# Key product by seven half products, with the activations held by halves of the tokens

## The chip, the cores and the metric

The kernel runs on one core of a Trainium2 chip. The metric is the device time of one execution in microseconds. It is taken without the profiler. Everything is computed in 32-bit floats; on TensorE one such matmul shows in the trace as two MATMUL records and two weight loads.

## The reference, cut to what matters

Four sequences (B = 4) of T = 512 tokens with H = 512 channels pass through an adaptive layer norm, an RWKV block (time mixing, then channel mixing), a second adaptive layer norm and a mixture of experts. The change lies in the channel mixing:

```python
h = _layer_norm(x, ln2_g, ln2_b)
hh = _time_shift(h)
kk = (h * cm_mk + hh * (1 - cm_mk)) @ Wkey.T        # 512 -> FF = 2048
kv = jax.nn.silu(kk) @ Wval.T                       # 2048 -> 512
sr = jax.nn.sigmoid((h * cm_mr + hh * (1 - cm_mr)) @ Wcr.T)
x = x + sr * kv
```

The key product is `kk`, the value product is `kv`.

## The kernel before, in words

**Order.** Each engine runs its instructions strictly in the order in which the Python source issues them. `weave(main, back)` sets that order: each time the main generator yields, one step of the back generator is put in. Around the change the main generator is `channel_mix(b)`, for b = 0 to 3, and the back generator is `channel_front(b + 1)` (norm, turn and mixes for the next sequence, 11 steps) followed by `channel_back(b - 1)` (second norm, router and slot tables of the previous sequence, 17 steps). At b = 0 there is only the front, at b = 3 only the back. Of the back's steps two are long on VectorE: step 13 picks the experts, and step 15 builds `at_slot` and `at_row`, which the matmuls of step 16 (`ps_rows`) read.

**Stages of channel_mix(b).** First come four gate products `ps_cr` with `wcr`; at b = 0 the four output products `o_steps(3)` of time mixing stand among them, and they begin with `flush()`, which issues the last division (`L364`, `L365`) on VectorE and, behind it, the last multiplication `av` (`L366`) on GpSimd. Then 16 chunks of 128 rows of f follow. `project` (`L323`) multiplies a chunk of `wkey` by the four tiles `xk` of 128 channels by 512 tokens: four matmuls of 512 columns into a bank `ps_kk`. ScalarE takes the sigmoid (`L541`), VectorE multiplies (`L542`) into the tile `s` of 512 tokens, and from chunk 8 on adds half of it to an earlier tile (`L546`). The banks of tag "ps" are four, so that a chunk may wait for three others before TensorE needs its bank again.

**The value product** is already made of seven products of halves, in `product` (`L562`), with three banks X, Y and Z, 32 MATMUL records of 256 columns each. The sums of the quarters of `wval` that it needs are made once, at b = 0, by `sum_step` (`L500`), one step in each chunk, and stored to `sums_d` (`L504`) for the later sequences. `minus` (`L576`) makes the differences of activations while the products run.

**Loads.** All DMAs except the gathers are issued by SyncE, in order, and an issue that has to wait holds up the ones behind it. Weights live in a pool of 8 tiles of 1 MB (`wpool`). `load_key` (`L94`) fetches 1 MB of `wkey` for four chunks, one group ahead; `get(0)`, called at f = 13, fetches the first quarter of `wval` for the value product.

Of the kernel before, what the change touches and what calls it, by code (L numbers as in the profile page):

```python
# [8 lines left out]
F32 = mybir.dt.float32  # L9
I32 = mybir.dt.int32  # L10
AF = mybir.ActivationFunctionType
# [3 lines left out]
P = 128  # L15
B, T, H = 4, 512, 512
NT = T // P
NK = H // P
FF = 4 * H
NF = FF // P  # L20
NG = FF // H
# [23 lines left out]
def adaln_block(  # L45
# [22 lines left out]
    nc = tc.nc  # L68
# [3 lines left out]
    wpool = ctx.enter_context(tc.tile_pool(name="w", bufs=8))  # L72
# [5 lines left out]
    def bank(name, tag="ps"):  # L78
        return psum.tile([P, 512], F32, tag=tag, name=name)

    def row_tile(name, shape=(P, H)):

        return tpool.tile(list(shape), F32, tag="t", name=name)
# [4 lines left out]
    def load_w(src, name, parts=1):  # L88

        w = w_tile(name)  # L90
        n = NK // parts
        rows = src.rearrange("(k p) o -> p k o", p=P)
        for i in range(parts):
            nc.sync.dma_start(w[:, i * n : (i + 1) * n, :], rows[:, i * n : (i + 1) * n, :])  # L94
        return w
# [224 lines left out]
    def project(w, acts, m, ps):  # L320

        for k in range(NK):
            nc.tensor.matmul(ps, w[:, k, m * P : (m + 1) * P], acts[k], start=(k == 0), stop=(k == NK - 1))  # L323
# [143 lines left out]

    h3_d = dram.tile([N, H], F32, tag="h3_d", name="h3_d")
    h3s = [None] * B
    wkey = {}  # L470


    HT, NF2 = T // 2, NF // 2
    (B11, B12, B21, B22, T1, T2, T3, T4) = range(8)
    sums_d = dram.tile([4, P, NF2 * HT], F32, tag="sums_d", name="sums_d")
    quarters, wsum = {}, {}

    def load_key(b, g):
        wkey[b, g] = load_w(wkey_t[:, g * H : (g + 1) * H], f"wkey_{b}_{g}")

    def load_quarter(b, q):
        w = wpool.tile([P, NF2, HT], F32, tag="w", name=f"wval_{b}_{q}")
# [7 lines left out]

    def sum_step(n):


        q, part = divmod(n, 4)
        if n == 0:
            for i in (B12, B11, B22, B21):
                wsum[i] = load_quarter(0, i)
        dst, one, other = ((B11, B12, B11), (B12, B22, B12), (B22, B22, B11), (B21, B21, B22))[q]
        at = slice(part * NF2 // 4, (part + 1) * NF2 // 4)
        nc.vector.tensor_sub(wsum[dst][:, at, :], wsum[one][:, at, :], wsum[other][:, at, :])  # L500
        if part == 3:
            i = (T1, T3, T2, T4)[q]
            quarters[0, i] = wsum[dst]
            nc.sync.dma_start(sums_d[i - T1].rearrange("p (k o) -> p k o", k=NF2), wsum[dst])  # L504

    def channel_mix(b):

        xk, xr = channel_mixes[b][CK], channel_mixes[b][CR]
        x1, ga = x1s[b], spread(GA, b)
        srs, xres = [], []  # L510
        for t in range(NT):
            ps = bank(f"ps_cr_{b}_{t}")
            project_tokens(wcr, xr, t, ps)
            yield
            sr = row_tile(f"sr_{b}_{t}")
            nc.scalar.activation(sr, ps, AF.Sigmoid)
            nc.gpsimd.tensor_mul(sr, sr, ga)
            srs.append(sr)
            if b == 0 and t == 1:
                yield from o_steps(B - 1)  # L520
            if t == 0:
                xres = [load_x(b, i, f"xr_{b}_{i}") for i in range(NT)]
            else:
                nc.gpsimd.tensor_mul(x1[t - 1], x1[t - 1], ga)
                nc.gpsimd.tensor_add(x1[t - 1], x1[t - 1], xres[t - 1])
        nc.gpsimd.tensor_mul(x1[NT - 1], x1[NT - 1], ga)
        nc.gpsimd.tensor_add(x1[NT - 1], x1[NT - 1], xres[NT - 1])

        ss = []
        order_of = (B11, T2, T1, B21, T3, B22, T4)  # L530

        def get(n):
            if n < len(order_of) and (b, order_of[n]) not in quarters:
                quarters[b, order_of[n]] = load_quarter(b, order_of[n])

        for f in range(NF):
            ps = bank(f"ps_kk_{b}_{f}")
            project(wkey[b, f // NK], xk, f % NK, ps)
            yield
            s = row_tile(f"s_{b}_{f}", (P, T))  # L540
            nc.scalar.activation(s, ps, AF.Sigmoid)  # L541
            nc.vector.tensor_mul(s, s, ps)  # L542
            ss.append(s)
            if f >= NF2:

                nc.vector.tensor_add(ss[f - NF2][:, HT:], ss[f - NF2][:, HT:], s[:, HT:])  # L546
            if b == 0:
                sum_step(f)
            if f % NK == 1 and f // NK + 1 < NG:
                load_key(b, f // NK + 1)  # L550
            if f >= NF - 4 and f % 2:
                get((f - NF + 3) // 2)

        def product(q, rows, col, ps, fresh, done=None):


            w = quarters.pop((b, q))
            for half in range(2):
                chunks = range(half * NF2 // 2, (half + 1) * NF2 // 2)
                for i in chunks:  # L560
                    for j in range(2):
                        nc.tensor.matmul(  # L562
                            ps[:, j * HT : (j + 1) * HT],
                            ss[rows + i][:, col + j * P : col + (j + 1) * P],
                            w[:, i, :],
                            start=(fresh and i == 0 and j == 0),
                            stop=(i == NF2 - 1 and j == 1),
                            skip_group_check=True,
                        )
                yield  # L570
                if done is not None:
                    for i in chunks:
                        done(i)

        def minus(dst, one, other):
            nc.vector.tensor_sub(dst, one, other)  # L576

        def result(t0, col, part):

            at = slice(col, col + HT)  # L580
            for j in range(2):
                t = t0 + j
                nc.vector.tensor_mul(srs[t][:, at], srs[t][:, at], part[:, j * HT : (j + 1) * HT])
                nc.vector.tensor_add(x1[t][:, at], x1[t][:, at], srs[t][:, at])


        X = bank(f"ps_x_{b}", "acc")
        get(2)
        yield from product(B11, 0, 0, X, True, lambda i: minus(ss[i][:, :HT], ss[i][:, HT:], ss[i][:, :HT]))
        c1 = row_tile(f"c1_{b}")  # L590
        nc.scalar.activation(c1, X, AF.Copy)

        Y = bank(f"ps_y_{b}", "acc")
        get(3)
        yield from product(T2, 0, 0, Y, True)
        u2 = row_tile(f"u2_{b}")
        nc.vector.tensor_add(u2, c1, Y)

        Z = bank(f"ps_z_{b}", "acc")
        get(4)  # L600
        yield from product(T1, 0, HT, Z, True, lambda i: minus(ss[i][:, HT:], ss[NF2 + i][:, HT:], ss[i][:, :HT]))
        c5 = row_tile(f"c5_{b}")
        nc.scalar.activation(c5, Z, AF.Copy)  # L603
        nc.gpsimd.tensor_add(c5, c5, c1)  # L604

        get(5)
        yield from product(
            B21, NF2, 0, X, False, lambda i: minus(ss[NF2 + i][:, :HT], ss[NF2 + i][:, :HT], ss[i][:, :HT])
        )
        result(0, 0, X)  # L610

        get(6)
        yield from product(T3, 0, HT, Y, False)
        nc.vector.tensor_add(c5, c5, Y)
        result(2, HT, c5)

        if b + 1 < B:
            load_key(b + 1, 0)
        yield from product(B22, NF2, 0, Z, False)
        nc.vector.tensor_add(u2, u2, Z)  # L620
        result(0, HT, u2)

        yield from product(T4, NF2, HT, Y, False)
        nc.vector.tensor_add(c1, c1, Y)
        result(2, 0, c1)
        channel_mixes[b] = None
# [444 lines left out]
    def weave(main, back, plan=()):  # L1071

        plan = iter(plan)
        for _ in main:
            for _ in range(next(plan, 1)):
                next(back, None)
# [5 lines left out]
    def chained(*parts):  # L1082
        for p in parts:
            yield from p()
# [42 lines left out]
    for b in range(1, B):  # L1127
        if b + 1 < B:
            back = chained(lambda: time_front(b + 1))
        else:  # L1130
            wcr = load_w(wcr_t, "wcr")
            load_key(0, 0)
            back = channel_front(0, "acc")
        weave(time_mix(b), back)
        drain(back)
    nc.sync.dma_start(router[:, :, :E_RT], w_router.rearrange("(k p) e -> p k e", p=P))
    for b in range(B):
        parts = []
        if b + 1 < B:
            parts.append(lambda: channel_front(b + 1, "ps"))  # L1140
        if b >= 1:
            parts.append(lambda: channel_back(b - 1))
        back = chained(*parts)
        weave(channel_mix(b), back)
        drain(back)
        if b == 0:
            clear_rest()
# [36 lines left out]
    for b in (B - 2, B - 1):  # L1184
        for t in range(NT):
            ps = down_bank(b, t)
# [51 lines left out]
```

## Time and profile before

| what | value |
| --- | --- |
| median of 3 runs | 1068.97 us (1068.79 to 1070.17) |
| the profiled execution, time | 1077.15 us |
| its span, first to last instruction | 1075.4 us |
| granted TensorE clock, mean | 0.988 |
| TensorE busy | 1043.0 us, 97% of the span |
| VectorE busy | 602.2 us, 56% |
| ScalarE busy | 284.0 us, 26% |
| GpSimd busy | 276.0 us, 26% |
| key products `ps_kk`, all four sequences | 225.4 us of TensorE |
| value products, ps_x + ps_y + ps_z | 57.3 + 84.8 + 57.0 us of TensorE |

The profiled execution is longer than the median by 8.2 us, so a sum made in the trace is compared with 1077.15 us, and only the difference is carried over to the median. In the rows of the trace "[1.19 <-DVE at_row L830]" says that the engine stood idle for 1.19 us before that row and that VectorE's instruction of line 830 ended the wait. "128x256 f32 x32" are 32 records of that shape. Line numbers of the profile are those of the kernel before.

In the trace the four key stages lie at 295 to 351, 413 to 473, 538 to 598 and 664 to 728 us from the start of the span, and each value stage follows its key stage.

### The profile page before, as it was taken

To read this page: it belongs to the slowest core of one execution; us is meant where nothing else is said; L and a number is where in the kernel's file an instruction comes from. 1 tells how busy PE (TensorE), PEld (TensorE's weight loads), DVE (VectorE), ACT (ScalarE), POOL (GpSimd) and SP (SyncE) were. 2 spreads that over 40 slices of the span, in tenths; PEclk is the share of its full clock that TensorE was granted. 3 is DMA by queue.
4 is the path that set the end of the run, shared out by engine and by line. 5 is a ranking of instruction groups with operands and counts; after the bars stand their busy time and mean duration, and the time that the engine had idled before them with its cause. 6 is when DMAs were issued, how large, how long until landed. Compare 5 with 4: busy or idle time off the path is not lost. (4 is left out here: it accounts for less than half of the span.)

```text
span 1075.4 us, 10261 instructions
## 1 busy us (share of the span) xinstructions
PE 1043.0 (97%) x3440; PEld 597.2 (56%) x3440; DVE 602.2 (56%) x1158; ACT 284.0 (26%) x459; POOL 276.0 (26%) x274
## 2 busy tenths in 40 slices
PE   7998989999999999999999999999999999999997
PEld 2443434444444884468644785448845666656643
DVE  5886998867464444747446576274456222224327
ACT  1744453534231004320152101311030222113210
POOL 2453463523430006100231006100013222141250
PEclk9998999999999999999999999999999999999999
DMA  8700130024024560084204611915242899899853
GB/s 313 236 1 2 39 99 0 1 84 135 27 78 157 171 230 1 29 316 134 59 1 150 232 40 41 347 43 190 65 156 84 283 381 382 302 320 311 290 181 109
DMA packets 93607, 161.77 MB, mean 150 GB/s; under 512 B 6552, under 2 KB 44952, under 8 KB 91504
## 3 DMA queue, kind: packets, MB, share of 16 engines
q1 hardware_dynamic: 87712, 141.95, 38.4%
q0 software_dynamic: 5840, 19.14, 5.6%
q8 instruction: 28, 0.46, 0.2%
q14 instruction: 27, 0.22, 0.1%
HBM read 136.11 MB, written 24.95 MB: 150 GB/s over the span
## 5 line engine op out<-in xcount | busy, mean ns | idle before, releaser
L323 PE MATMUL ps_kk<-mix_ln,wkey 128*128 128x512 f32 x512 | 225.4, 596 | 0.0
L323 PEld LDWEIGHTS ps_kk<-mix_ln,wkey 128*128 128x128 f32 x512 | 96.3, 191 | 114.1 <-issue 112.2
L202 POOL TENSOR_TENSOR rstd_ln<-rstd_ln,minus_half 128x1 f32<-128x1 f32 x64 | 40.0, 625 | 232.9 <-DVE rstd_ln L201 220.4
L542 DVE TENSOR_TENSOR s<-s,ps_kk 128x512 f32<-128x512 f32 x64 | 44.0, 687 | 99.4 <-ACT s L541 99.3
L562 PE MATMUL ps_y<-wval,s 128*128 128x256 f32 x384 | 84.8, 379 | 0.0
L541 ACT ACTIVATE s<-ps_kk 128x512 f32<-128x512 f32 x64 | 38.2, 597 | 158.8 <-PE ps_kk L323 153.1
L1009 PE MATMUL ps_down<-wrt,at 128*128 128x512 f32 x164 | 78.9, 604 | 1.0 <-issue 1.0
L993 PE MATMUL ps_up<-wrt,xt 128*128 128x256 f32 x328 | 77.9, 380 | 1.3 <-DVE xt L987 1.3
L562 PEld LDWEIGHTS ps_y<-wval,s 128*128 128x128 f32 x384 | 72.8, 190 | 9.8
L246 DVE SCALAR_TENSOR_TENSOR mix_ln<-hT_ln,inv,mix_ln 128x511 f32<-128x511 f32 x64 | 61.7, 1006 | 24.2 <-ACT mix_ln L240 24.2
L970 POOL DMA_INDIRECT xg<-h_d,token x41 | 39.3, 959 | 126.4 <-PE ps_down L1009 42.6
L328 PE MATMUL ps_o<-wo,av 128*128 128x512 f32 x128 | 59.5, 619 | 4.7 <-POOL av L366 4.1
L993 PEld LDWEIGHTS ps_up<-wrt,xt 128*128 128x128 f32 x328 | 59.1, 190 | 8.8 <-DVE xt L987 2.4
L604 POOL TENSOR_TENSOR c<-c,c 128x512 f32<-128x512 f32 x4 | 5.1, 1286 | 226.2 <-ACT c L603 184.4
L323 PE MATMUL ps_r<-mix_ln,wr 128*128 128x512 f32 x128 | 59.3, 607 | 0.1
L987 DVE COPY xt<-ps_xt 128x512 f32<-128x512 f32 x41 | 28.3, 689 | 55.0 <-PE ps_xt L985 43.1
L323 PE MATMUL ps_v<-mix_ln,wv 128*128 128x512 f32 x128 | 58.1, 597 | 0.0
L562 PE MATMUL ps_x<-wval,s 128*128 128x256 f32 x256 | 57.3, 380 | 0.0
L915 PE MATMUL ps_up_sh<-h,wsh 128*128 128x512 f32 x128 | 57.2, 593 | 0.0
L562 PE MATMUL ps_z<-wval,s 128*128 128x256 f32 x256 | 57.0, 379 | 0.0
L929 PE MATMUL ps_down_sh<-wsh,mid 128*128 128x512 f32 x128 | 56.3, 594 | 0.4 <-PEq L1180 0.4
L328 PE MATMUL ps_cr<-wcr,mix_ln 128*128 128x512 f32 x128 | 55.9, 592 | 0.0
(195 smaller groups left out, 1487.3 us busy)
## 6 DMA issues: line engine op xcount, KB each, us to landing
wrt<-in_rt_up_dram SPq DMA_DIRECT2D x41, 512.0 KB
wrt<-in_rt_down_dram SPq DMA_DIRECT2D x41, 512.0 KB
wkey<-in_wkey_t_dram SPq DMA_DIRECT2D x16, 1024.0 KB
wval<-in_wval_t_dram SPq DMA_DIRECT2D x16, 1024.0 KB
wval<-sums_d SPq DMA_DIRECT2D x12, 1024.0 KB
y_d<-y SPq DMA_DIRECT2D x41, 256.0 KB
mod<-mod_d SPq DMA_DIRECT2D x22, 256.0 KB
x<-in_x_dram SPq DMA_DIRECT2D x16, 256.0 KB
```

The costliest lines, as they stand in the source:

```text
L202: nc.gpsimd.tensor_tensor(rstd, rstd, minus_half, ALU.pow)
L246: nc.vector.scalar_tensor_tensor(t[:, 1:], hT[:, : T - 1], inv[:, m - MK, k : k + 1], t[:, 1:], ALU.mult, ALU.add)
L323: nc.tensor.matmul(ps, w[:, k, m * P : (m + 1) * P], acts[k], start=(k == 0), stop=(k == NK - 1))
L328: nc.tensor.matmul(ps, acts[k][:, t * P : (t + 1) * P], w[:, k, :], start=(k == 0), stop=(k == NK - 1))
L541: nc.scalar.activation(s, ps, AF.Sigmoid)
L542: nc.vector.tensor_mul(s, s, ps)
L562: nc.tensor.matmul(ps[:, j * HT : (j + 1) * HT], ss[rows + i][:, col + j * P : col + (j + 1) * P], w[:, i, :], start=(fresh and i == 0 and ...
L915: nc.tensor.matmul(ps, wu[:, k, m * P : (m + 1) * P], h3s[b][k], start=(k == 0), stop=(k == NK - 1))
L929: nc.tensor.matmul(ps, mids[b][j][:, t * P : (t + 1) * P], shared[j // ND][1][:, j % ND, :], start=(j == 0), stop=(j == len(mids[b]) - 1),)
L970: nc.gpsimd.indirect_dma_start(out=xg, out_offset=None, in_=h3_d, in_offset=bass.IndirectOffsetOnAxis(ap=token[:, s : s + 1], axis=0),)
L993: nc.tensor.matmul(ps[:, :D], xt[:, k, :], wu[:, k, :], start=(k == 0), stop=(k == NK - 1))
L1009: nc.tensor.matmul(ps, at[:, j, :], wd[:, j, :], start=(j == 0), stop=(j == ND - 1))
```

## The change

The key product is also made by seven products of halves (half of the channels, half of the tokens, half of f). Two chunks of each half of f make a pair, and there are four pairs; in a pair each of the seven products is four matmuls of 256 columns that fill both halves of one bank. The products go into three banks X, Y and Z; four results (`a11`, `a12`, `a21`, `a22`, each 128 x 512) come out of a pair. They are the activations of one half of the tokens and one half of f, where before a tile held all tokens of one chunk.

The sums of weights (`S1` to `S4`) are made at b = 0 by `key_sums(p)` and stored to `keys_d`; later sequences load seven blocks, 1.75 MB a pair, from there. The sums of activations (`T1` to `T4`) are made by `key_terms` among the gate products. Silu is done by `silu`: sigmoid on ScalarE, the multiplication on VectorE for `a11` and `a12` and on GpSimd for `a22` and `a21`. The last product of a pair, `A22 T4`, is put off (`late`) until after the first product of the next pair, and that of the last pair into the middle of the first value product.

`channel_mix` now yields three times in a pair, 12 times in the key stage, where it yielded 16 times. The value product and its order are the same, with the tiles renamed (`B11` to `Q11` and so on) and each `minus` over 512 columns.

The diff, cut to its core:

```diff
+    keys_d = dram.tile([N_PAIR, P, 7 * H], F32, tag="keys_d", name="keys_d")
+    def load_keys(b, p):
+        lo = wpool.tile([P, 4, H], F32, tag="w", name=f"keys_{b}_{p}_lo")
+        hi = wpool.tile([P, 4, H], F32, tag="w", name=f"keys_{b}_{p}_hi")
...
+        if b == 0:
+            for i, f, h in ((A11, 0, 0), (A12, 0, 1), (S3, 1, 0), (A22, 1, 1)):
+                at = f * (FF // 2) + p * HT
+                rows = wkey_t[h * HT : (h + 1) * HT, at : at + HT]
+                nc.sync.dma_start(keys[b, p][i], rows.rearrange("(k p) f -> p k f", p=P))
+        else:
+            nc.sync.dma_start(lo, keys_d[p, :, : 4 * H].rearrange("p (i o) -> p i o", i=4))
+            nc.sync.dma_start(hi[:, :3, :], keys_d[p, :, 4 * H :].rearrange("p (i o) -> p i o", i=3))
+    def key_sums(p):
+        k = keys[0, p]
+        nc.vector.tensor_add(k[S1], k[S3], k[A22])
+        nc.vector.tensor_sub(k[S2], k[S1], k[A11])
+        nc.vector.tensor_sub(k[S3], k[A11], k[S3])
+        nc.vector.tensor_sub(k[S4], k[A12], k[S2])
+        lo, hi = loaded.pop(p)
+        nc.sync.dma_start(keys_d[p, :, : 4 * H].rearrange("p (i o) -> p i o", i=4), lo)
+        nc.sync.dma_start(keys_d[p, :, 4 * H :].rearrange("p (i o) -> p i o", i=3), hi[:, :3, :])
...
         for t in range(NT):
             ps = bank(f"ps_cr_{b}_{t}")
...
+            key_terms(t)
...
-        for f in range(NF):
-            ps = bank(f"ps_kk_{b}_{f}")
-            project(wkey[b, f // NK], xk, f % NK, ps)
-            yield
-            s = row_tile(f"s_{b}_{f}", (P, T))
-            nc.scalar.activation(s, ps, AF.Sigmoid)
-            nc.vector.tensor_mul(s, s, ps)
-            ss.append(s)
-            if f >= NF2:
-                nc.vector.tensor_add(ss[f - NF2][:, HT:], ss[f - NF2][:, HT:], s[:, HT:])
-            if b == 0:
-                sum_step(f)
-            if f % NK == 1 and f // NK + 1 < NG:
-                load_key(b, f // NK + 1)
-            if f >= NF - 4 and f % 2:
-                get((f - NF + 3) // 2)
+        def last_product(p, k, Y, c1):
+            def do():
+                key_product(Y, k[A22], terms["T4"], False)
+                nc.vector.tensor_add(c1, c1, Y)
+                a12[p] = silu(c1, f"a12_{p}", nc.vector)
+                nc.vector.tensor_add(a21[p], a21[p], a22[p])
+            return do
+        late = None
+        for p in range(N_PAIR):
+            k = keys.pop((b, p))
+            X = bank(f"ps_kx_{b}_{p}", "acc")
+            key_product(X, k[A11], B11, True)
+            c1 = copied(f"kc1_{p}", X)
+            if late is not None:
+                late()
+            if p + 1 < N_PAIR:
+                loaded[p + 1] = load_keys(b, p + 1)
+            Y = bank(f"ps_ky_{b}_{p}", "acc")
+            key_product(Y, k[S2], terms["T2"], True)
+            yield
+            u2 = row_tile(f"ku_{b}_{p}")
+            nc.vector.tensor_add(u2, c1, Y)
+            Z = bank(f"ps_kz_{b}_{p}", "acc")
+            key_product(Z, k[S1], terms["T1"], True)
+            c5 = copied(f"kc5_{p}", Z)
+            nc.gpsimd.tensor_add(c5, c5, c1)
+            key_product(X, k[A12], B21, False)
+            if b == 0:
+                sum_step(4 * p)
+            yield
+            a11[p] = silu(X, f"a11_{p}", nc.vector)
+            key_product(Y, k[S3], terms["T3"], False)
+            nc.vector.tensor_add(c5, c5, Y)
+            key_product(Z, k[S4], B22, False)
+            if b == 0:
+                sum_step(4 * p + 1)
+            yield
+            a22[p] = silu(c5, f"a22_{p}", nc.gpsimd)
+            nc.vector.tensor_add(u2, u2, Z)
+            a21[p] = silu(u2, f"a21_{p}", nc.gpsimd)
+            if b == 0:
+                if p + 1 < N_PAIR:
+                    key_sums(p + 1)
+                sum_step(4 * p + 2), sum_step(4 * p + 3)
+            late = last_product(p, k, Y, c1)
+            if p == N_PAIR - 1:
+                get(0)
+                get(1)
...
-        yield from product(B11, 0, 0, X, True, lambda i: minus(ss[i][:, :HT], ss[i][:, HT:], ss[i][:, :HT]))
-        c1 = row_tile(f"c1_{b}")
-        nc.scalar.activation(c1, X, AF.Copy)
+        yield from product(Q11, a11, X, True, minus(a11, a21, a11), late)
+        c1 = copied("c1", X)
...
         if b + 1 < B:
-            load_key(b + 1, 0)
+            load_keys(b + 1, 0)
...
             wcr = load_w(wcr_t, "wcr")
-            load_key(0, 0)
+            loaded[0] = load_keys(0, 0)
...
         back = chained(*parts)
+        if b == 0:
+            key_sums(0)
         weave(channel_mix(b), back)
```

`copied` copies a bank to SBUF on ScalarE; `key_product` is the loop of four matmuls. The last hunk puts `key_sums(0)` ahead of `channel_mix(0)`.

## The prediction

> **What bounds the kernel now.** I read the page first (busy time and the slices), then TensorE's timeline in the key and value stages, then those of VectorE, GpSimd and SyncE there.
>
> ```profile
> PE 1043.0 (97%) x3440; PEld 597.2 (56%) x3440; DVE 602.2 (56%) x1158; ACT 284.0 (26%) x459; POOL 276.0 (26%) x274
> PEclk9998999999999999999999999999999999999999
> 435.57 24.20 PE L323 MATMUL ps_kk<-mix_ln,wkey 128*128 128x512 f32 x56
> 459.61 1.04 PE L229 MATMUL ps_t_ln<-ident,h3r 128*128 128x128 f32 x8
> 358.04 7.07 PE L562 MATMUL ps_y<-wval,s 128*128 128x256 f32 x32
> 364.95 7.07 PE L562 MATMUL ps_z<-wval,s 128*128 128x256 f32 x32
> ```
>
> TensorE is the bound, at full clock, with hardly a gap. From start to start, 56 records of 512 columns take 24.04 us, 429 ns each; 32 of 256 columns take 6.91 us, 216 ns. So a 256-column record costs half, weight load included.
>
> ```profile
> 276.32 11.43 PE L328 MATMUL ps_o<-wo,av 128*128 128x512 f32 x26 [0.68 <-POOL av L366]
> 275.00 1.26 POOL L366 TENSOR_TENSOR av<-av,p 128x512 f32<-128x512 f32 x1
> 270.09 3.35 DVE L365 RECIPROCAL p<-p 128x512 f32<-128x512 f32 x1
> 300.49 1.17 DVE L500 TENSOR_TENSOR wval<-wval,wval 128x512 f32<-128x512 f32 x1
> 305.52 0.68 DVE L500 TENSOR_TENSOR wval<-wval,wval 128x512 f32<-128x512 f32 x1
> 340.01 0.34 SPq L504 DMA_DIRECT2D sums_d<-wval  x1
> 340.44 0.39 SPq L488 DMA_DIRECT2D wval<-in_wval_t_dram  x1
> DMA  0000000009990999989837999999995000000010
> 710.39 2.72 PE L838 MATMUL ps_rows<-at_slot,at_row 128*128 128x47 f32 x16 [1.19 <-DVE at_row L830]
> 713.00:716.00 3.00, 3.00 (x5) 1.37 (x5) 2.84 (x8) 0.00 (x0) 0.00 (x0) 0.53 0.05 22
> ```
>
> Five things to see. The last division already stops TensorE at 276. A subtraction of two SBUF tiles takes 0.68 us, but 1.17 beside a busy GpSimd. A 1 MB store and the 1 MB load behind it (340.01, 340.44; the DMA row is 338 to 350 in slices of 0.3 us) end at 347.2, 7.2 us after the store's issue. TensorE waits for `at_row`. And after that wait and its thin matmuls the clock fell to 0.53 for 3 us, 1.7 us lost (`ps_kk`'s 32 records behind it take 15.44 us instead of 13.7).
>
> **The change part by part.**
>
> *TensorE's work.* Removed: 512 records at 429 ns, 219.8 us. Added: 4 sequences x 4 pairs x 7 products x 8 records = 896 at 216 ns, 193.4 us. **-26.4 us**, 1.65 a pair. A product is 1.73 us, a pair 12.1 us.
>
> *Added elementwise work in a pair.* VectorE: seven operations at 0.69 us (before: four, and two halves at 0.42), 4.8 us; ScalarE two copies and four sigmoids at 0.60, 3.6 us; GpSimd three at 1.27 us, 3.8 us. All fit beside 12.1 us in sum; `key_terms`, 8 x 0.42 us, fits beside the 13.5 us of gate products. But order counts. With a pair's start as 0: X ends at 1.7, the late product of the pair before at 3.45, Y 5.2, Z 6.9, X again 8.6, Y again 10.4, Z again 12.1. The second Y product needs `u2 = c1 + Y` by 8.6. Ahead of it on VectorE stand the late `c1` addition (3.65 to 4.35), the multiplication of `a12` behind its sigmoid (5.1 to 5.8), the addition to `a21` (6.5), and the back's step. So `u2` ends at 7.2, and a back step of over 1.4 us there stops TensorE. The other waits (`c5`, Z's bank) have 2.5 us and more. Before, four banks gave some 10 us.
>
> *Batch 0, start.* `key_sums(0)` and two `key_terms` stand ahead of the last division on VectorE. From 265.4: four sums at 1.0 (between 0.68 and 1.17, GpSimd is busy) 4.2 us with gaps, four half terms 1.7; the 1.85 us that VectorE idled there are used up. The reciprocal ends near 277.4, not 273.4. On SyncE the two stores of `key_sums(0)` now stand ahead of the load `mod_2_0`, so GpSimd, which needs it for the two `sr` before `av`, starts them at 275.4 (1.75 MB at the 390 GB/s of the DMA rows, 4.5 us). `av` ends at 279.7 either way: **+3.5**, TensorE idle 4.2. The `wval` and key loads move back too, to 276, 7 us and more ahead of use.
>
> *Batch 0, pairs.* Pair 0 is crowded by the front's mixes (1.7 us each there): `u2` and `c5` 0.3 late each, **+0.6**. `key_sums(1)` comes behind two mixes and Z's addition, so S2 is ready near 18.9 where TensorE wants it at 15.4: **+3.6**. After it follow S3, S4, two `sum_step`, `c1`, `a12`, `a21`, `u2`: 1.5 late in pair 1, 0.8 and 1.1 in pairs 2 and 3: **+3.4**. `keys_0_2` and `keys_0_3` queue behind 2.75 MB of stores and land some 1 us before VectorE needs them at the latest; I charge nothing, 2 us each if that cover goes.
>
> *Batch 0, first value load.* Before, `get(0)` went out 10.7 us ahead of its product. Now it stands on SyncE behind the last store to `sums_d`, which waits for `sum_step(15)`, which waits on VectorE for the pair's last Z. From Z's end: 0.15 + 0.69 + 2 x 0.68 + 0.15 = 2.35 us to the store's issue, then 7.0 to the landing (low end 4.3, if the load did not have to wait for the store): **+9.3**. Queued behind the load are only quarters used 20 us later.
>
> *Batches 1 and 2.* Step `channel_back` 3 (statistics and a modulation, 2.5 us) falls at the tight place of pair 3: +1.15. The store `h3r_0_1` waits for it and holds `get(0)` on SyncE: issue at 9.5, 1.25 MB, landing 14.3, wanted at 13.2: +1.1. The first `minus` behind the late product: +0.3. Four back steps move from the key into the value stage; step 15 still has two half products, 6.9 us, before `ps_rows`, as it had: nothing, with 2 us at stake if VectorE comes to it late. The pair loads, 1.75 MB in 12.1 us or 145 GB/s, are issued a pair ahead: nothing. **+2.5 each.**
>
> *Batch 3.* Step 15 (8.8 us of VectorE at 491 to 500, here 9.7 with the later batches' few more) starts only at 9.1 of pair 3 and ends at 18.8; `ps_rows` stands at 12.7 and ends at 19.0. It cost 2.9 us over its work before, 5.4 now: +2.5. Steps 12 and 13: +0.6. Step 17 (2.8 us) stands ahead of the first `minus`, which the second value product needs: +3.3. **+6.4.**
>
> *The clock.* The row shows 1.7 us lost after a wait of 1.19 us and 2.7 us of thin matmuls. The Trainium skill's page "TensorE: Matmul & The Clock Gate", section "HAM oscillation — how this bites in real kernels", speaks against this change: only gaps over some 3.4 us drop the clock, but each then costs half of a cold stretch. By the rule three gaps here count (4.2, 3.6, 9.3), 5.1 us, of which 1.4 hide in the waits behind the second; by the row the four or five shorter waits count too, 6.8 to 8.5 more. I take the rule, **+3.7**, since a dense stream stands around the short waits and 0.68 us at 276 dropped nothing (row PEclk).
>
> Sum of the waits: 3.5 + 0.6 + 3.6 + 3.4 + 9.3 + 2 x 2.5 + 6.4 + 3.7 = 35.5; less 26.4: **+9.1 us**. In the profiled execution 1077.15 becomes 1086.2; the median 1068.97 becomes 1078.1.
>
> **The rivals.**
>
> *Main case, 0.50*: as summed, 1078, on its own 1071 to 1085.
>
> *Faster, 0.15*: VectorE keeps up. Its place is the `u2` addition. If its neighbours run at 0.68 rather than 1.0 to 1.7 us, and the back's long steps start earlier than I place them, batches 1 to 3 keep their 6.6 us each, 19.8; batch 0 pays 20.4 less 3 for uncontended sums, and gains 6.6: net -9, 1060. It decides once all waits together stay under 24.3 us. For it: VectorE is 56% busy. Against: the batch 0 load is a matter of order on SyncE, not of speed.
>
> *Much slower, 0.20*: the clock falls at each wait, as the row at 713 allows, and `keys_0_2`, `keys_0_3` come late: 35.5 + 8.5 + 4 - 26.4 = +21.6, 1091.
>
> *It cancels, 0.15*: no drop of the clock (-3.7), load in 4.3 us (-2.7), sums at 0.68 (-3): 35.5 - 9.4 - 26.4 = -0.3, 1069, as easily somewhat slower.
>
> That the change does not do what it says is excluded for the products: the built program holds the 448 matmuls of 256 columns, two records each.
>
> **How the numbers follow.** 0.2% is 2.1 us, about what a measurement of this kernel can tell from no change. Slower: 0.50 + 0.20 + 0.06 of the last case, 0.76; same 0.09; faster 0.15. The predicted time is the main case's. The range from 1061 to 1091 leaves out half of the fast and half of the much slower case.
>
> **What would show it.** Key products at 216 ns a record, TensorE's busy time down. A wait of some 4 us at `ps_o` ended by `av`; one of 3 to 4 us at `ps_ky` of pair 1 ended by `key_sums`; one of 9 us ahead of batch 0's first `ps_x`, ended by a DMA, followed by 3 us at half clock; in batch 3 `ps_rows` and `ps_y` waiting for VectorE. I am wrong if the records take clearly over 216 ns, if batch 0's first `ps_x` does not wait, or if batches 1 and 2 wait over 4 us each.

## The result, and the profile after

The changed kernel takes 1086.78 us (median of 4 runs, 1086.04 to 1089.46); run beside it, the kernel before takes 1069.18. The ratio is 1.0168, 95% interval 1.0148 to 1.0187: **17.6 us slower**, where +9.1 was forecast. The sign is right, the size is not. The profiled execution spans 1087.8 us, 12.4 more than that of before. The two medians lie further apart than the two profiled executions, because that of before was 8.2 us above its median and that of the changed kernel 2.7 above: at 86 us and between 824 and 840 us, outside the change, the older one had waits and half clock that most of the other profiles do not have.

From the page of the changed kernel, the engines' busy time and the granted clock in 40 slices:

```profile
PE 1025.3 (94%) x3824; PEld 673.8 (62%) x3824; DVE 645.3 (59%) x1174; ACT 303.0 (28%) x491; POOL 343.9 (32%) x322
PEclk9999999999899899999999999998999999999999
```

TensorE's busy time fell by 17.7 us, though the work removed is 26.4: part of what is left runs at half clock (the mean granted clock is 0.977, before 0.988). A slice is 27.2 us; the three 8s of the PEclk row are the slices that begin at 272, 354 and 734 us. TensorE's timeline shows what lies there, with the wait ahead of a group in brackets and what ended it:

```profile
279.54 13.35 PE L328 MATMUL ps_o<-wo,av 128*128 128x512 f32 x26 [6.12 <-POOL av L366]
318.17 1.97 PE L599 MATMUL ps_ky<-T,keys_lo 128*128 128x256 f32 x8 [2.41 <-DVE keys_lo L507]
325.81 1.99 PE L599 MATMUL ps_ky<-T,keys_hi 128*128 128x256 f32 x8 [2.22 <-DVE ku L638]
344.06 1.97 PE L599 MATMUL ps_kx<-mix_ln,keys_lo 128*128 128x256 f32 x8 [1.65 <-DMA keys_lo<-in_wkey_t_dram]
368.68 5.43 PE L675 MATMUL ps_x<-wval,a 128*128 128x256 f32 x16 [11.71 <-DMA wval<-in_wval_t_dram]
480.27 1.99 PE L599 MATMUL ps_ky<-T,keys_hi 128*128 128x256 f32 x8 [0.65 <-DVE ku L638]
485.74 3.69 PE L675 MATMUL ps_x<-wval,a 128*128 128x256 f32 x16 [1.75 <-DMA wval<-in_wval_t_dram]
731.13 3.65 PE L949 MATMUL ps_rows<-at_slot,at_row 128*128 128x47 f32 x16 [2.90 <-DVE at_row L941]
748.47 10.12 PE L675 MATMUL ps_y<-wval,a 128*128 128x256 f32 x32 [3.61 <-issue]
```

Where nothing waits, a key product of 8 records takes 1.73 us from start to start (shown as 1.89, with the modelled end), as forecast. The long waits stand where they were forecast. The last row names no releaser ("issue" means that the profile shows none), but VectorE's timeline has one: the differences that this product needs (`minus`, `L691`) begin at 747.68, behind the back's step 17.

```profile
744.45 0.55 DVE L972 TENSOR_TENSOR behind<-ends,ramp 1x384 f32<-1x384 f32 x1
747.68 2.49 DVE L691 TENSOR_TENSOR a<-a,a 128x512 f32<-128x512 f32 x4
```

And some groups are slow in themselves: 26 records of `ps_o` in 13.35 us (11.43 before), 16 of `ps_x` in 5.43 (3.69 in batch 1), 32 of `ps_y` in 10.12 (7.07 elsewhere), 16 of `ps_rows` in 3.65 (2.72 before, 1.88 in batch 1 where nothing waits). The clock in those places, from the table of windows (busy times by engine, then granted clock, DMA share, GB/s):

```profile
279.00:282.00 3.00, 2.46 (x3) 1.17 (x4) 0.34 (x1) 0.14 (x1) 1.00 (x2) 0.50 1.09 348
731.00:734.00 3.00, 2.87 (x14) 2.87 (x14) 3.00 (x11) 0.00 (x0) 0.00 (x0) 0.50 0.00 0
748.00:751.00 3.00, 2.54 (x6) 2.12 (x7) 2.17 (x4) 0.00 (x0) 0.00 (x0) 0.50 0.83 229
```

Half clock, each time behind a wait.

A ledger from the starts of groups in the two timelines. "Gate" is from a batch's first `ps_cr` to its first key product, with batch 3's output projection in batch 0's; "key and value" is the rest of the batch. For batches 1 to 3 only the rest is given; their gate products take 13.73 us in both kernels:

| stage | before, us | after, us | difference | with the 6.6 us saved taken out |
|---|---|---|---|---|
| gate, batch 0 | 29.29 | 36.65 | +7.36 | +7.36 |
| key and value, batch 0 | 104.16 | 120.34 | +16.18 | +22.8 |
| key and value, batch 1 | 111.36 | 106.97 | -4.39 | +2.2 |
| key and value, batch 2 | 111.96 | 107.51 | -4.45 | +2.1 |
| key and value, batch 3 | 112.51 | 116.47 | +3.96 | +10.6 |
| sum | | | +18.66 | +45.1 |

Batch 0's +22.8 is made of 9.0 in the pairs (the key stage is 68.21 us; its work 47.5, from the 55.82 of before less 6.6 and less the 1.73 of the late product; the load 11.7), 11.7 at the load, and 2.1 in the value products behind it (52.13 against 48.34 and the late product), 1.8 of them half clock in the first 16 records.

The whole stretch, from batch 0's first gate product to the first shared product, is 510.49 us before and 529.13 after. It is used below as the measure of each experiment as well, since outside it nothing is changed; the times of one kernel on the three chips of the experiments spread by 0.6 to 0.7% on each (the kernel before: 1064 to 1075 us over all three). Ratios are to the kernel before on the same chip.

### The profile page after: what moved, and what is told of

It is laid out like the page before. It is cut to its first block, busy times and chain, and to the rows that moved or that the text cites. A ratio compares the mean times of both kernels' runs of the same rounds, so it can differ in the third digit from the quotient of the medians.

```text
span 1087.8 us, 11259 instructions
## 1 busy us (share of the span) xinstructions
PE 1025.3 (94%) x3824; PEld 673.8 (62%) x3824; DVE 645.3 (59%) x1174; ACT 303.0 (28%) x491; POOL 343.9 (32%) x322
## 5 line engine op out<-in xcount | busy, mean ns | idle before, releaser
L675 PE MATMUL ps_y<-wval,a 128*128 128x256 f32 x384 | 88.4, 389 | 3.6 <-issue 3.6
L675 PEld LDWEIGHTS ps_y<-wval,a 128*128 128x128 f32 x384 | 74.6, 196 | 14.8 <-issue 4.4
L675 PE MATMUL ps_x<-wval,a 128*128 128x256 f32 x256 | 60.7, 395 | 15.1 <-DMA wval<-in_wval_t_dram 15.1
L599 PE MATMUL ps_ky<-T,keys_hi 128*128 128x256 f32 x256 | 61.5, 383 | 4.1 <-DVE ku L638 3.7
L675 PEld LDWEIGHTS ps_x<-wval,a 128*128 128x128 f32 x256 | 50.3, 199 | 23.3 <-issue 16.3
L599 PE MATMUL ps_kx<-mix_ln,keys_lo 128*128 128x256 f32 x256 | 60.6, 379 | 1.6 <-DMA keys_lo<-in_wkey_t_dram 1.6
L675 PE MATMUL ps_z<-wval,a 128*128 128x256 f32 x256 | 57.3, 380 | 0.0
L599 PEld LDWEIGHTS ps_ky<-T,keys_hi 128*128 128x128 f32 x256 | 47.5, 190 | 14.2 <-DVE ku L638 6.6
L222 ACT ACTIVATE xn_ln<-x,nm_ln,rstd_ln 128x512 f32<-128x512 f32 x32 | 25.7, 811 | 102.4 <-DVE nm_ln L215 102.4
```

Source lines behind the costliest of these rows:

```text
L599: nc.tensor.matmul(ps[:, c * HT : (c + 1) * HT], w[:, k, c * P : (c + 1) * P], acts[k], start=(fresh and c == 0 and k == 0), stop=(c == 1 ...
L675: nc.tensor.matmul(ps[:, j * HT : (j + 1) * HT], acts[p][:, c, j * P : (j + 1) * P], w[:, i, :], start=(fresh and i == 0 and j == 0), stop ...
```

## The experiments

Theory: the 26.4 us saved are real, and 45 us of waits, with half clock behind the longer ones, eat them; the waits come from where things stand in a queue. Its rivals: the records behind a wait are slow because their operands drip in; or VectorE and the transfers are simply too loaded in batch 0, wherever the work stands.

**1. The load of Q11 earlier.**

```diff
+            if p == N_PAIR - 1:
+                get(0)
             if p + 1 < N_PAIR:
                 loaded[p + 1] = load_keys(b, p + 1)
```

> The load of Q11 is issued at the start of the fourth pair (before the last two sums and the last store to sums_d; in batches 1 and 2 before the h3 stores), nothing else moves. Theory A (the waits of 11.7 us in batch 0 and of 1.75 and 1.68 us in batches 1 and 2 ahead of the first ps_x are matters of order on SyncE): in batch 0 the load goes out near 350 us instead of 360.7, lands near 357 to 358, the wait falls from 11.7 to under 2 us, and with it the 2 us of half clock behind it; the two short waits vanish. 9.7 + 2 + 3.4 = 15 us less than the changed kernel, about 1072 us. Rival B (the transfers ahead of it, 2.75 MB of stores, hold the load up wherever it is issued): the load, among the stores of keys_d and sums_d, lands 3 us before it does now at the best, wait 8 us, clock still falls; about 1080 us.

Measured: 1076.85 us, ratio to before 1.0064 (1.0032 to 1.0097); the stretch 514.42 us, 14.7 less than the changed kernel. Its TensorE timeline, then SyncE's:

```profile
357.29 3.04 PE L677 MATMUL ps_x<-wval,a 128*128 128x256 f32 x13 [3.11 <-DMA wval<-in_wval_t_dram]
```

```profile
347.19 0.39 SPq L541 DMA_DIRECT2D sums_d<-wval  x1
347.68 1.15 SPq L526 DMA_DIRECT2D wval<-in_wval_t_dram  x1
```

The first row is cut off by the end of its view; all 16 records take 3.69 us. The wait falls from 11.71 to 3.11, the half clock behind it is gone in this execution (edit 8 has it again), and the 1.75 and 1.68 us of batches 1 and 2 vanish. Most of the wait was a matter of order on SyncE; theory A holds with a remainder of 3 us. The 2.75 MB of stores ahead of the load are the likely cause of it, which this run does not show.

**2. key_sums(0) behind the output projection.**

```diff
                 yield from o_steps(B - 1)
+                key_sums(0)
...
-        if b == 0:
-            key_sums(0)
         weave(channel_mix(b), back)
```

> key_sums(0) and its two stores stand behind the last output projection (o_steps of batch 3), not ahead of it; nothing else moves. Theory A (ps_o waits because the four sums stand ahead of the last division on VectorE and their stores ahead of mod_2_0 on SyncE): the wait of 6.12 us at ps_o falls to 0.7 to 1.5 and the half clock behind it (13.35 us for 26 records instead of 11.43) goes: 5 + 1.9 = 7 us less than the changed kernel, about 1080 us; the sums, with GpSimd idle, take 0.69 us each. Rival B (it is the key_terms on VectorE, or the loads on the queue, that make av late): the wait stays over 3 us and the total moves by less than 3 us.

Measured: 1089.33 us, 1.0154 (1.0108 to 1.0200), nothing gained; the stretch 527.37, 1.8 less. Yet the gate stage is 30.46 us instead of 36.65, as theory A said. What was gained there was lost later. The timelines of TensorE, SyncE and VectorE, in this order:

```profile
277.51 11.43 PE L328 MATMUL ps_o<-wo,av 128*128 128x512 f32 x26 [1.85 <-POOL av L366]
316.85 3.49 PE L600 MATMUL ps_ky<-T,keys_lo 128*128 128x256 f32 x8 [2.96 <-DVE keys_lo L507]
```

```profile
291.01 0.33 SPq L511 DMA_DIRECT2D keys_d<-keys_lo  x1
296.61 9.02 SPq L526 DMA_DIRECT2D wval<-in_wval_t_dram  x4
```

```profile
290.29 0.69 DVE L507 TENSOR_TENSOR keys_lo<-keys_lo 128x512 f32<-128x512 f32 x1
308.63 0.69 DVE L537 TENSOR_TENSOR wval<-wval,wval 128x512 f32<-128x512 f32 x1 [4.05 <-DMA wval<-in_wval_t_dram]
```

The sums stand in program order behind the last token tile's addition, so their stores leave at 291, and the loads that are queued behind them on SyncE (pair 1's keys, then 4 MB of quarters) at 292 to 297. The first `sum_step` then waits 4.05 us for its quarter and holds VectorE's queue, and pair 1's S2 is later than ever. With GpSimd idle a sum takes 0.69 us. The key stage grows by 3.6 us, the half clock in it (8 records in 3.49 us) included; batch 0's value products and batch 1 lose another 3.2. Batch 3, which the edit does not touch, takes 2.3 less, since more of it ran at full clock. The cause of the wait at `ps_o` is shown, though not how much of it is VectorE and how much SyncE, since both moved; a move that takes a queue's later entries along is no repair.

**3. The waits filled.** Products of `ident` and `ones` into a spare bank, ahead of what waits (cut; the comments say where each call stands):

```diff
+    def filler(n, name):
+        ps = bank(f"ps_fill_{name}")
+        for i in range(n):
+            nc.tensor.matmul(ps, ident, ones, start=(i == 0), stop=(i == n - 1))
...
+            filler(13, "x")     # batch 0, ahead of the first ps_x
+            filler(4, "y")      # batch 3, ahead of the first ps_y
+            filler(3, "rows")   # batch 3, ahead of ps_rows
+                    filler(6, "o")   # ahead of the last av product
```

> Matrix products whose result is used nowhere are put into the four long waits of TensorE: 6 (12 records of 429 ns, 5.1 us) ahead of the last av product, 13 (11.2 us) ahead of batch 0's first ps_x, 3 (2.6 us) ahead of batch 3's wait for at_row, 4 (3.4 us) ahead of batch 3's first ps_y. Nothing that the kernel waits for comes earlier. Theory A (the slow records behind those waits are slow because the clock fell): all of them run at 216 or 429 ns again; ps_o -1.9, ps_x -2.0, batch 3 (ps_rows 1.7, ps_x 1.5, ps_y 3.0) -6.3, together 10 us less than the changed kernel, about 1077 us, and granted clock 0.99. Rival B (the records behind a wait are slow because their operands come one by one: the load in parts, the differences of VectorE): nothing gained, at most 2 us lost where the filling is longer than the wait; 1087 to 1089 us.

Measured: 1080.79 us, 1.0100 (1.0063 to 1.0137); the profiled span is 1077.0 us instead of 1087.8, the stretch 519.90, 9.2 less, at a mean clock of 0.994. TensorE's timeline:

```profile
276.47 11.43 PE L405 MATMUL ps_o<-wo,av 128*128 128x512 f32 x26 [0.89 <-POOL av L371]
363.80 3.69 PE L683 MATMUL ps_x<-wval,a 128*128 128x256 f32 x16 [0.57 <-DMA wval<-in_wval_t_dram]
724.40 2.48 PE L963 MATMUL ps_rows<-at_slot,at_row 128*128 128x47 f32 x16 [0.33 <-DVE at_row L953]
739.20 7.14 PE L683 MATMUL ps_y<-wval,a 128*128 128x256 f32 x32 [0.19 <-issue]
```

No operand comes earlier, yet the same records run at full speed (11.43, 3.69 and 7.14 us). So the clock, not dripping operands, made them slow: useless work in the waits is worth 9 us of the stretch. It is no luck of one execution: in the four profiles that keep the wait of some 6 us at `ps_o` (the changed kernel, edits 1, 4 and 8) its 26 records take 12.91 to 14.03 us. Rival B is out, but for `ps_rows`: at a granted clock of 1.00 it still takes 2.48 us here against 1.88 where nothing waits, so 0.6 us of its slowness is `at_row` coming piece by piece. That is most of what was missing in batch 3, where 6.3 us were expected back and 5.5 came.

**4. Batch 3's back later**, as it stands in batches 1 and 2:

```diff
-        weave(channel_mix(b), back)
+        weave(channel_mix(b), back, (0,) * 11 if b == B - 1 else ())
```

> In batch 3 the back's first step is run at the twelfth yield, as in batches 1 and 2 where the front's steps stand ahead of it; nothing else moves. Theory A (batch 3 loses because the back's steps 15 and 17 fall into the last pair and ahead of the first differences): at_row and ps_y wait no more, the clock does not fall there; batch 3 takes 108 us as batches 1 and 2 do, not 116.5: 8.5 us less than the changed kernel, about 1078 us. Rival B (VectorE has too much to do in batch 3 wherever the steps stand, or the routing that ends later holds up the shared products and the first slots): the time moves by under 3 us, with waits in the value products or behind 793 us.

Measured: 1081.39 us, 1.0113 (1.0076 to 1.0149); the stretch 518.97. Batch 3 falls from 116.47 to 105.7 us, 10.8 less, with no wait for `at_row` and none of 3.61 us at `ps_y`. Theory A holds, and somewhat better than expected; behind batch 3 only a wait of 1.27 us is new.

**5. Batch 0's weight sums rearranged.** The loads go out first, the sums run in VectorE's gaps between the projection's token tiles:

```diff
+        if b == 0:
+            loaded[1] = load_keys(0, 1)
+            for i in (Q12, Q11):
+                wsum[i] = load_quarter(0, i)
         for t in range(NT):
...
+                for i, _ in enumerate(o_steps(B - 1)):
+                    if i == 1:
+                        key_terms(0), key_terms(1)
+                    if i > 1:
+                        key_sums(i - 2), store_keys(i - 2)
+                    yield
+                wsum[Q22] = load_quarter(0, Q22)
...
+                if 1 <= p < N_PAIR - 1:
+                    key_sums(p + 1), store_keys(p + 1)
+                if p == 2:
+                    wsum[Q21] = load_quarter(0, Q21)
                 sum_step(4 * p + 1)
...
-                if p + 1 < N_PAIR:
-                    key_sums(p + 1)
```

> Batch 0's weight sums alone are moved: the loads of pair 1's keys and of two quarters go out ahead of the last output projection, the first two key_terms and key_sums(0), key_sums(1) run between its four token tiles, where VectorE stood idle; the later key_sums run one segment of a pair earlier, and the fourth quarter is loaded only at pair 2, so that the keys of pairs 2 and 3 find their buffers free some 7 us earlier. The late load of Q11 and batch 3 stay as in the changed kernel. Theory A (the waits at ps_o and in batch 0's pairs come from where the sums, their loads and their stores stand, not from their amount): ps_o waits under 1.5 us at full clock (-6.5), the 8.8 us of waits in batch 0's key products fall under 3 us (-6), the 11.7 us at the first ps_x stay: 12 us less than the changed kernel, about 1075 us. Rival B (in batch 0 VectorE and the 14 MB of loads and stores are too much for the 49 us of the key products wherever they stand): waits of 6 us and more stay in the pairs, as when key_sums(0) alone was moved; at most 6 us less, 1081.

Measured: 1079.92 us, 1.0106 (1.0074 to 1.0139); the stretch 519.15, 10 less. TensorE:

```profile
272.77 11.43 PE L328 MATMUL ps_o<-wo,av 128*128 128x512 f32 x26 [0.68 <-POOL av L366]
326.72 1.99 PE L609 MATMUL ps_ky<-T,keys_hi 128*128 128x256 f32 x8 [1.79 <-DVE ku L648]
358.64 1.62 PE L687 MATMUL ps_x<-wval,a 128*128 128x256 f32 x3 [13.60 <-DMA wval<-in_wval_t_dram]
```

The gate stage is 29.29 us, that of the kernel before to the hundredth. The key stage gives less: the waits in the pairs fall only from 9.0 to 5.8 us (those of pair 1 go, but two of 1.79 at `u2` come in pairs 2 and 3, where it was 0.4 each), and the load takes 1.9 back, 13.60 instead of 11.71 (its row is cut off by the end of its view; all 16 records take 5.70 us, at half clock again). It is between the two theories: the start is all order, the pairs are so in part.

**6. All three together**, edits 1, 4 and 5:

> The three moves together: the load of Q11 at the start of the fourth pair, the back of batch 3 begun at the twelfth yield, the weight sums of batch 0 as in e5_keys_ahead. Theory A (the matrix work saved, 26.4 us, is real, and what ate it were waits of order and the clock behind them): about 12 (batch 0's sums) + 15.5 (load) + 8.5 (batch 3) = 36 us less than the changed kernel, about 1051 us and so 18 us faster than the kernel before; granted clock 0.99. Rival B (the waits shift: with the short waits gone, the next transfer or VectorE's chain in a pair binds): over 1060 us, with new waits of over 5 us in sum in batches 0 to 3.

Measured: **1053.45 us, 0.9853 (0.9822 to 0.9883), faster than the kernel before**; the stretch 494.78. That is 34.4 us less than the changed kernel, where 36 was expected. Left over in batch 0 are the two waits of 1.8 us at `u2` and 4.59 at the load with 2.0 us of half clock behind it; in each later batch 0.65 at `u2`.

**7. Edit 4 on the kernel before.**

> The kernel before, with batch 3's back begun at the twelfth yield too. Theory A: it loses its wait of 1.19 us for at_row in batch 3 and the 2.5 us of half clock there: 3 to 4 us faster than the kernel before, about 1066 us; so most of what the same edit gives the changed kernel (9 us) is the return of what the change had made worse. Rival B: the kernel before gains as much, 8 us, and the edit says nothing about the change.

Measured: 1066.76 us, 0.9989 (0.9970 to 1.0007): no difference that can be told, the stretch 509.86 instead of 510.49. I had expected 3 to 4 us. The wait shrinks as expected, but in its TensorE timeline and windows:

```profile
747.74 2.48 PE L838 MATMUL ps_rows<-at_slot,at_row 128*128 128x47 f32 x16 [0.54 <-DVE at_row L830]
750.04 5.39 PE L562 MATMUL ps_x<-wval,s 128*128 128x256 f32 x16
```

```profile
751.00:754.00 3.00, 3.00 (x10) 2.39 (x9) 2.90 (x10) 0.00 (x0) 0.00 (x0) 0.58 0.00 0
```

Even 0.54 us of wait and 2.5 us of products of 47 columns were followed by half clock here. It is no rule: in batch 2 of the kernel before the same sequence was followed by full clock (its TensorE timeline; the 16 records behind take 3.70 us, not 5.39):

```profile
623.72 2.48 PE L838 MATMUL ps_rows<-at_slot,at_row 128*128 128x47 f32 x16 [0.55 <-DVE at_row L830]
626.02 3.70 PE L562 MATMUL ps_x<-wval,s 128*128 128x256 f32 x16
```

The comparison of the changed kernel's better versions is not tilted by this edit: the kernel before has next to nothing from it.

**8. Edits 1 and 4**, batch 0's sums left alone:

> The early load of Q11 and the later back of batch 3 together, batch 0's sums left as they are in the changed kernel. Theory A (the losses are separate places and add up): 15.5 + 8.5 = 24 us less than the changed kernel, about 1063 us, 6 us faster than the kernel before. Rival B (later waits take over part of it): over 1070 us.

Measured: 1062.99 us, 0.9939 (0.9920 to 0.9959). The stretch is 504.93, 24.2 less than the changed kernel; the two alone gave 14.7 and 10.2. They add up to within 0.7 us, but that is in part chance. The load wait is much as in edit 1, 3.25 us, yet here half clock follows it, 2.9 us in the value products of batch 0 that edit 1 did not pay; and batch 3 gains 1.9 more than in edit 4, since its own load wait goes too. TensorE's timeline:

```profile
359.66 6.60 PE L677 MATMUL ps_x<-wval,a 128*128 128x256 f32 x16 [3.25 <-DMA wval<-in_wval_t_dram]
```

**9. u2 first.** In edit 6, `late` is split: product, addition to `c1` and sigmoid as before, the rest behind `u2`:

```diff
             nc.vector.tensor_add(u2, c1, Y)
+            if rest is not None:
+                rest()       # a12's multiplication, a21 += a22
```

> e6_all with one change of order on VectorE: the multiplication of a12 and the addition to a21 of the pair before stand behind u2 = c1 + Y, not ahead of it. Theory A (u2 waits for what stands ahead of it in the queue, 1.3 us of these two and up to 1.8 beside a busy GpSimd): the waits at the second ps_ky, 1.79 and 1.78 us in batch 0 and 0.65 us in each later batch, vanish: 5.5 us less than e6_all, about 1048 us. Rival B (u2 is late for its own inputs, the copy c1 by ScalarE or the Y product): the waits stay, 1053 us.

Measured: 1051.52 us, 0.9845 (0.9815 to 0.9876); the stretch 493.36, 1.4 less than edit 6, where 5.5 was expected. TensorE:

```profile
329.61 1.97 PE L609 MATMUL ps_kx<-mix_ln,keys_lo 128*128 128x256 f32 x8 [1.39 <-DMA keys_lo<-in_wkey_t_dram]
349.48 6.68 PE L696 MATMUL ps_x<-wval,a 128*128 128x256 f32 x16 [6.65 <-DMA wval<-in_wval_t_dram]
```

The waits of 1.79, 1.78 and 0.65 us at `u2` are gone (0.17 is left in pair 0), so it was late for what stood ahead of it. In batches 1 to 3 each key stage is 0.9 us shorter. In batch 0 it is the same to 0.02 us: what was won was waited away at the transfers, 1.39 us for keys and 6.65 instead of 4.59 for Q11, which lands at 349 in both kernels.

**10. The load sooner still.** In edit 9, Q11 takes the buffer that Q21 had, in the third pair:

```diff
-                    key_sums(p + 1), store_keys(p + 1)
-                if p == 2:
-                    wsum[Q21] = load_quarter(0, Q21)
+                    key_sums(p + 1)
+                    if p == 1:
+                        store_keys(p + 1)
+                    else:
+                        get(0)
```

with Q21 and pair 3's stores behind it at the start of the fourth pair, and the four sums of T4 among the value products.

> e9_u2_first, and in batch 0 the load of Q11 goes out in the third pair, ahead of the fourth quarter's load and of the stores of pair 3's keys; the four sums of T4 move into the value products. Theory A (the 4.59 us still lost at the first ps_x are the 3.75 MB of other transfers ahead of the load): the wait vanishes and the 1.9 us of half clock behind it too: 6.5 us less than e9_u2_first, about 1042 us. Rival B (the transfers pushed back, or the four sums in the value products, make a later product wait): at most 3 us gained.

Measured: **1041.77 us, 0.9758 (0.9728 to 0.9788)**, 27 us below the median of the kernel before beside it (1068.79); the stretch 483.51, 27.0 less than before. From its page, then TensorE's timeline:

```profile
PE 1009.3 (97%) x3824; PEld 666.2 (64%) x3824; DVE 641.8 (62%) x1174; ACT 301.2 (29%) x490; POOL 341.5 (33%) x322
PEclk9999999999999999999999999999999999999999
```

```profile
341.57 3.62 PE L703 MATMUL ps_x<-wval,a 128*128 128x256 f32 x16
```

No wait at the load, no half clock; 3.6 us of waits remain in batch 0's pairs. It is 9.8 us less than edit 9, where 6.5 was expected: the wait at the load had grown to 6.65 there and the half clock behind it to 3.1. The stretch has lost what TensorE's work has lost, 26.4 us, and half a microsecond more. TensorE and VectorE run as many instructions as in the changed kernel (3824 and 1174), so the rival that batch 0 is too loaded wherever the work stands is out. Load and sums were moved together here; what each gives alone is not shown.

## Why the prediction was right in sign and wrong in size

Its places were right, but for two waits at `u2` in batch 0 (pairs 2 and 3) that hardly came; the terms of its sum, with what the ledger gives for each:

| term | forecast, us | measured, us |
|---|---|---|
| TensorE's work | -26.4 | -26.4 |
| batch 0, wait at `ps_o` | +3.5 | +5.4 |
| batch 0, waits in the pairs (0.6 + 3.6 + 3.4) | +7.6 | +9.0 |
| batch 0, first value load | +9.3 | +11.7 |
| half clock in batch 0 | +3.7 | +4.0 |
| batches 1 and 2 | +5.0 | +4.3 |
| batch 3 | +6.4 | +10.6 |
| sum | +9.1 | +18.7 |

**Batch 3 is the step that failed most**, by 4.2 us, and it is the clock. The waits came nearly as said: 2.90 us at `ps_rows`, and 3.61 at `ps_y`, where 3.3 was forecast. The half clock behind them was charged at nothing, because of the choice of the Trainium skill's rule ("TensorE: Matmul & The Clock Gate", "HAM oscillation — how this bites in real kernels": gaps over some 3.4 us) over the row of the trace, which showed the clock at 0.53 after 1.19 us and thin products. What it cost can be told from edit 2, whose batch 3 is the same and where `ps_rows` kept its clock behind the same wait:

```profile
733.94 2.48 PE L950 MATMUL ps_rows<-at_slot,at_row 128*128 128x47 f32 x16 [2.91 <-DVE at_row L942]
```

From start to start that is 2.3 us, against 3.4 in the changed kernel. So the half clock cost 1.1 us in `ps_rows`, 1.5 in the `ps_x` records behind and 3.0 in `ps_y`, 5.7 in all; the kernel before, reckoned in the same way, paid 1.8 here, so 3.9 net. The list of gaps was short even by the rule: `ps_y`'s 3.61 us is over it, and the 3.3 forecast for that wait was too near the bound to be left out. Edit 3 shows that it is the clock, edit 4 that the back's steps bring the waits. The size is that of one execution: with batch 3's instructions unchanged, edits 1, 2 and 5 have 116.7, 114.2 and 115.2 us there (116.5 in the table), so the step was 2 to 4 us short.

**The start of batch 0** was 1.9 us too small. The sums ran beside GpSimd and were taken at 1.0 us each. VectorE's timeline in the changed kernel, then GpSimd's:

```profile
263.14 1.50 DVE L506 TENSOR_TENSOR keys_lo<-keys_hi 128x512 f32<-128x512 f32 x1
264.67 1.64 DVE L507 TENSOR_TENSOR keys_lo<-keys_lo 128x512 f32<-128x512 f32 x1
266.23 1.75 DVE L508 TENSOR_TENSOR keys_hi<-keys_lo,keys_hi 128x512 f32<-128x512 f32 x1
```

```profile
264.05 1.71 POOL L353 TENSOR_TENSOR p<-e,e 128x512 f32<-128x512 f32 x1
275.27 1.26 POOL L568 TENSOR_TENSOR sr<-sr,mod 128x512 f32<-128x512 f32 x1 [4.94 <-DMA mod<-mod_d]
278.23 1.26 POOL L366 TENSOR_TENSOR av<-av,p 128x512 f32<-128x512 f32 x1
```

Three of the four took 1.5 to 1.75 us, more than the upper end of my bounds (1.17); together they took 5.4 us, not 4.2. GpSimd then waited for `mod_2_0`, as forecast, until 6.7 us after the end of the sums, where the prediction's times give 5.8. The reciprocal was done at 276.0, and `av` came only behind the two `sr`. So the path through SyncE set the end, as in the prediction, but both its links were longer. (Clock times in the two profiles are not to be compared here: this stage begins 2.2 us earlier in the changed kernel's.)

**The first value load** was 2.4 us too small, in two parts. The last store waits for two sums taken at 0.68 us each; GpSimd's multiplication at 358.4 to 359.7 ran beside them, and they took 2.65 together. So the store went out at 360.29, 3.5 us after the last Z, not 2.35. From there to TensorE's start it was 8.4 us, not 7.0. VectorE, then SyncE:

```profile
357.61 2.65 DVE L537 TENSOR_TENSOR wval<-wval,wval 128x512 f32<-128x512 f32 x2
```

```profile
349.98 10.62 SPq L541 DMA_DIRECT2D sums_d<-wval  x2
360.66 1.64 SPq L526 DMA_DIRECT2D wval<-in_wval_t_dram  x2
```

**The pairs of batch 0**: S2 of pair 1 came 2.6 us late, not 3.6. `u2` in pair 1 was 2.4 late, not 1.5, since the addition ahead of it took 1.75 us; in pairs 2 and 3 it was 0.4 late each, not 0.8 and 1.1. And `keys_0_3`, charged at nothing with 2 us at stake, cost 1.9. The half clock of batch 0 was right to 0.3 us, though from two gaps and not three: none followed the wait for S2, and the others cost about 2 us each, not 1.7.

**Batches 1 and 2** were right to 0.4 us each, in part by luck: the wait at `u2` was 0.65 us, not 1.15, that at the load 1.75 and 1.68, not 1.1. The places by which the prediction said that it could be judged, a wait at `ps_o` ended by `av`, one at `ps_ky` of pair 1 ended by `key_sums`, one ahead of the first `ps_x` ended by a DMA, and batch 3 waiting for VectorE, all came. Of the rivals, "much slower" was the nearer one at +21.6: its half clock at shorter waits came in batch 3 but not at the 2.41 and 2.22 us in batch 0's pairs.

## What to carry to other kernels

The matrix work that a substitution saves can be lost to the order of what it adds: here the same arithmetic is worth +17.6 or -27 us by order alone, and the saving arrived in full only once the sums stood where VectorE was idle and the needed loads left ahead of the stores. Price each wait on a busy TensorE with the half clock that may follow it, and price vector work that runs beside GpSimd at the contended duration (1.5 to 1.75 us here, not 0.68). When a wait is taken away, ask what the engine meets next at the new time: in edit 9 a transfer that landed at the same time as before took back all that was gained ahead of it.

## What the runs showed of the hardware that was not expected

Whether a short wait costs clock varies between executions of the same instructions. The wait for `keys_lo` in pair 1 of batch 0 is 2.41 us in the changed kernel, in edit 4 and in edit 8; from TensorE's timelines of edit 4 and edit 8, beside the changed kernel's row at 318.17 with 1.97 us for the eight records:

```profile
316.99 3.65 PE L599 MATMUL ps_ky<-T,keys_lo 128*128 128x256 f32 x8 [2.41 <-DVE keys_lo L507]
```

```profile
318.10 3.48 PE L599 MATMUL ps_ky<-T,keys_lo 128*128 128x256 f32 x8 [2.41 <-DVE keys_lo L507]
```

The same eight records, the same wait, nearly twice the time (in edits 1 and 3 they take 1.97 as well). It cost nothing in the end: TensorE had a wait of 2.22 us at `u2` next (325.81), and in edits 4 and 8 that wait is gone, since VectorE caught up meanwhile. The key stage of edit 4 is 67.86 us, that of the changed kernel 68.21. In edit 4's timeline, the group that waited:

```profile
323.93 1.89 PE L599 MATMUL ps_ky<-T,keys_hi 128*128 128x256 f32 x8
```

Executions differ in the same way at 83 us, ahead of anything that was changed: behind waits of 2.83 and some 0.7 to 0.9 us, eight records of 512 columns took 6.43 us in the profile of before and 3.70 in that of the changed kernel, which is 2.7 us between two executions of the same instructions. It fits a clock that is judged over stretches that start independently of the program, as the same page of the Trainium skill says of its window (section "Part 1: The HAM clock gate (the "warmup" mystery)"); no run here shows where those stretches begin. For a sum it means that a wait of 2 to 3 us has a chance of half clock, not a certainty in either direction, and that half clock ahead of another wait may cost nothing.
